# Spectral layer in three parts of 4, 2 and 2 channel blocks instead of two halves

## Chip, cores and metric

The kernel runs on one core of a Trainium2 chip. The metric is the device time of one execution in microseconds (us); the figure for a kernel is the median of its runs. Times inside an execution are counted from the start of the profiled span.

## What is computed

The input is an image of 48 x 48 tokens with 768 channels, in float32. Layer 0 is a transformer block (attention with relative positions, then an MLP). Layer 1, which the change touches, filters in the frequency domain, separately in 8 blocks of 96 channels. Cut to what matters:

```
xf = rfft2(x, axes=(1, 2), norm='ortho')          # 48 x 25 frequencies
xf = xf.reshape(B, H, Wh, 8, 96)
o1r = relu(mm(xr, w1[0]) - mm(xi, w1[1]) + b1[0])  # per block, 96 x 96
o1i = relu(mm(xi, w1[0]) + mm(xr, w1[1]) + b1[1])
o2r = softshrink(mm(o1r, w2[0]) - mm(o1i, w2[1]) + b2[0], 0.01)
o2i = softshrink(mm(o1i, w2[0]) + mm(o1r, w2[1]) + b2[1], 0.01)
y = irfft2((o2r + 1j * o2i).reshape(B, H, Wh, C), s=(H, W), norm='ortho')
return y + x
```

Blocks of channels do not mix, so the layer may be worked on in any groups of blocks. All frequencies of a block have to be there before its last transform along the rows.

## The kernel before

All Fourier transforms are matmuls with constant matrices. They run in four steps, with two trips through scratch memory in DRAM.

**Rows forward** (`rows_forward`, lines 1069 to 1087) runs at the end of each of the three passes `p` of the MLP. It multiplies the tokens in `x1` by `rows_dft` into PSUM (`zp`), copies them to an SBUF tile `zt` (eight buffers, 100 partitions x 384), and writes each `zt` to `z1[k]`, where `k` is the half of the channels. In the first two passes ScalarE makes the copies; in the last pass VectorE and ScalarE take turns (`balanced_copy`, lines 73 to 77). In the last pass the loads of the first two units (below) are issued between the writes of the two halves.

**Units** (`class Unit`, lines 1180 to 1279). The spectral part is cut into 14 units: two halves of 4 channel blocks, each with 7 groups of up to 4 column frequencies `k` (25 in all, so that the last unit of a half has only one). A unit passes through a load and four stages:

- `load`: `load_frequencies` (line 937) brings two `zi` tiles from `z1`, two frequencies each.
- `columns(i)`, frequency `i`: one matmul for each block into `fp`, and a copy to `xf` (VectorE for even `i`, ScalarE for odd).
- `first(i)`, block `i`: VectorE adds real and imaginary part (`both`), three 192-wide matmuls go into `lp` and `l1`, ScalarE copies `l1` (`p_both`), VectorE adds it (`pre`), ScalarE applies the relu (`o1`), and GpSimd writes a negated copy next to it.
- `second(i)`, frequency `i`: two matmuls for each block into `mp2`, VectorE adds the bias (`zz`) and clamps (`cl`), GpSimd subtracts `cl` from `zz`.
- `back(i)`, frequency `i`: one matmul into `yp`, as wide as the half (384), a copy to `y`; after each second frequency `y` is written to `z2`.

**Rows back** (`rows_back`, lines 1281 to 1297) is a generator for one half and one of six groups `g` of rows. Its first step loads `zo` (100 partitions, three buffers) from `z2`; each of the next three steps, called pieces here, makes two matmuls into `rps`, adds `x1` on VectorE into `yt` (four buffers), and writes `yt` to the output.

**Order.** The loop at line 1308 goes through rounds `r`, and in each round through steps `i` of 0 to 3. In a step stand `back` of unit `r-3`, `second` of `r-2`, `first` of `r-1` and `columns` of `r`, so four units are under way at once. From round 12 each step also advances the row generators of the first half: 20 of their 24 steps lie in the rounds, the other four behind the loop, and then come the six groups of the second half, one after the other. This order is binding for TensorE alone (`manual_schedule` at line 1306). The queues of the other engines, and that of SyncE, which issues all transfers of this part, are ordered by the framework; each runs its own queue in order. The framework also makes an instruction wait until a buffer it needs is free.

In the trace a float32 matmul has two records, so the 72 matmuls of the row step show as `x144`.

Of the kernel before, what the change touches and what calls it, by code (L numbers as in the profile page):

```python
# [9 lines left out]
F32 = mybir.dt.float32  # L10
# [3 lines left out]
ALU = mybir.AluOpType  # L14
# [4 lines left out]
P = 128  # L19
HW = 48  # L20
T = HW * HW
# [8 lines left out]
G = 384  # L30
NB = 8
BS = C // NB
CH = C // 2
KW = HW // 2 + 1
LAM = 0.01
LOW = -3.0e38
# [8 lines left out]
def block_then_afno(  # L45
# [25 lines left out]
    nc = tc.nc  # L71

    def balanced_copy(i, dst, src):
        if i % 2:
            nc.scalar.copy(dst, src)
        else:
            nc.vector.tensor_copy(dst, src)
# [14 lines left out]
    dram = ctx.enter_context(tc.tile_pool(name="scratch", bufs=1, space=DRAM))  # L92

    z1 = [dram.tile([HW * 2 * KW, CH], F32, name=f"z1_{k}") for k in range(2)]
    z2 = [dram.tile([HW * 2 * KW, CH], F32, name=f"z2_{k}") for k in range(2)]
    q_d = [dram.tile([P, T], F32, name=f"q_d{i}") for i in range(NC)]
    k_d = [dram.tile([P, T], F32, name=f"k_d{i}") for i in range(NC)]
    v_d = dram.tile([T, C], F32, name="v_d")
# [6 lines left out]
    x1 = main.rearrange("p (t c) -> p t c", t=NT)  # L105
# [83 lines left out]
    with ExitStack() as flag_scope:  # L189
# [11 lines left out]
        with ExitStack() as att:  # L201
# [336 lines left out]
            with tc.manual_schedule(engines={mybir.EngineType.PE, mybir.EngineType.SP}):  # L538
# [3 lines left out]
                psum = att.enter_context(tc.tile_pool(name="ps_att", bufs=1, space=PSUM))  # L542
# [76 lines left out]
                with tc.manual_schedule(engines={mybir.EngineType.Activation}):  # L619
                    for n, (pr, c, u) in enumerate(runs):  # L620
# [111 lines left out]
        with tc.If(safe < 1):  # L732
            with ExitStack() as att:
# [27 lines left out]
                for pr in range(NC):  # L761
                    w3 = []
                    for n, name in enumerate(("g_wq", "g_wk", "g_wv")):
                        w = w_pool.tile([P, NC, P], F32, name=name)
                        nc.sync.dma_start(
                            out=w,
# [167 lines left out]
    turn = ctx.enter_context(tc.tile_pool(name="turn", bufs=6))  # L934
    first_loads = []

    def load_frequencies(half, k0):

        rows = z1[half].rearrange("(r k) c -> r k c", k=KW)
        tiles = []  # L940
        for k in range(k0, min(k0 + 4, KW), 2):
            n = min(2, KW - k)
            zi = turn.tile([P, C], F32, name="zi", tag="turn")
            zi = zi[: 2 * HW].rearrange("p (k c) -> p k c", c=CH)
            nc.sync.dma_start(out=zi[:, :n], in_=rows[:, k : k + n, :])
            tiles.append(zi)
        return tiles

    with ExitStack() as mlp:
# [119 lines left out]
        def rows_forward(p):  # L1069

            for k in range(2):
                for g in (2 * p, 2 * p + 1):
                    for a, parts in enumerate(((0,), (1, 2), (3, 4), (5,))):
                        zp = psum.tile([2 * 2 * KW, CH], F32, name="zp", tag=f"o{a}")
                        for b in parts:
                            nc.tensor.matmul(  # L1076
                                zp, rows_dft[:, b, :], x1[:, 3 * g + b // 2, ts(k, CH)],
                                start=(b == parts[0]), stop=(b == parts[-1]),
                            )
                        zt = turn.tile([2 * 2 * KW, CH], F32, name="zt", bufs=8)  # L1080
                        if p < 2:
                            nc.scalar.copy(zt, zp)
                        else:
                            balanced_copy(a, zt, zp)
                        nc.sync.dma_start(out=z1[k][ts(4 * g + a, 4 * KW), :], in_=zt)
                if (p, k) == (2, 0):
                    first_loads.extend(load_frequencies(0, k0) for k0 in (0, 4))
# [39 lines left out]
    with ExitStack() as sp:  # L1127
# [44 lines left out]
        nc.vector.tensor_tensor(a1e, a1e, a1[:, 0], ALU.subtract)  # L1172

        z2_h = [z.rearrange("(r k) c -> r k c", k=KW) for z in z2]
        NBH = NB // 2

        def by_k(a):
            return a.rearrange("p (k h) -> p k h", h=HW)
# [1 line left out]
        class Unit:  # L1180
# [1 line left out]

            def __init__(self, half, k0):
                self.half, self.k0 = half, k0
                self.nk = min(4, KW - k0)
                self.n = self.nk * HW
                self.zz = []

            def load(self):
                self.zi = first_loads.pop(0) if first_loads else load_frequencies(self.half, self.k0)

            def columns(self, i):

                if i == 0:
                    self.xf = mid.tile([BS, NBH, 2, 4, HW], F32, name="xf")
                if i >= self.nk:
                    return
                fp = psum.tile([BS, NBH, 2, HW], F32, name="fp", tag="f")  # L1200
                for b in range(NBH):
                    nc.tensor.matmul(  # L1202
                        fp[:, b].rearrange("p t h -> p (t h)"), self.zi[i // 2][:, i % 2, ts(b, BS)], cols,
                        start=True, stop=True,
                    )
                balanced_copy(i, self.xf[:, :, :, i, :], fp)

            def first(self, i):

                if i == 0:  # L1210

                    self.o1 = mid.tile([BS, NBH, 4, 3, HW], F32, name="o1")
                b = NBH * self.half + i
                re, im = (
                    self.xf[:, i, t, : self.nk, :].rearrange("p k h -> p (k h)") for t in range(2)
                )
# [25 lines left out]
            def second(self, i):  # L1242

                if i >= self.nk:
                    return
                zz = mid.tile([2 * HW, NBH, BS], F32, name="zz", bufs=10)
                self.zz.append(zz)
                blocks_at = NBH * self.half
                mp = psum.tile([2 * HW, NBH, BS], F32, name="mp2", tag="m")
                for e in range(NBH):  # L1250
                    for t in range(2):
                        nc.tensor.matmul(  # L1252
                            mp[:, e], self.o1[:, e, i, 1 - t : 3 - t].rearrange("p t h -> p (t h)"),
                            a2[:, blocks_at + e, t], start=(t == 0), stop=(t == 1),
                        )
                nc.vector.tensor_tensor(zz, mp, d2[:, ds(blocks_at, NBH)], ALU.add)

                flat = zz.rearrange("p n o -> p (n o)")
                cl = mid.tile([2 * HW, CH], F32, name="cl", bufs=3)
                nc.vector.tensor_scalar(cl, flat, LAM, -LAM, ALU.min, ALU.max)  # L1260
                nc.gpsimd.tensor_tensor(flat, flat, cl, ALU.subtract)

            def back(self, i):

                if i >= self.nk:
                    return
                zz = self.zz[i]
                if i % 2 == 0:
                    self.y = mid.tile([2 * HW, 2, CH], F32, name="y", bufs=3)
                yp = psum.tile([2 * HW, CH], F32, name="yp", tag="y", bufs=1)  # L1270
                nc.tensor.matmul(  # L1271
                    yp, icols, zz.rearrange("p n o -> p (n o)"), start=True, stop=True
                )
                balanced_copy(i, self.y[:, i % 2, :], yp)
                if i % 2 or i == self.nk - 1:
                    n = i % 2 + 1
                    nc.sync.dma_start(
                        out=z2_h[self.half][:, ds(self.k0 + i + 1 - n, n), :], in_=self.y[:, :n]
                    )

        def rows_back(half, g):

            zo = zin.tile([4 * KW, 4, CH], F32, name="zo", bufs=3)
            nc.sync.dma_start(
                out=zo, in_=z2[half][ts(g, 16 * KW), :].rearrange("(a p) c -> p a c", a=4)
            )
            yield
            for i in range(3):
                yt = mid.tile([P, CH], F32, name="yt", bufs=4)
                rp = psum.tile([P, CH], F32, name="rps", tag="f")  # L1290
                for e in range(2):
                    nc.tensor.matmul(  # L1292
                        rp, irows[:, 2 * i + e, :], zo[:, i + e, :], start=(e == 0), stop=(e == 1)
                    )
                nc.vector.tensor_tensor(yt, rp, x1[:, 3 * g + i, ts(half, CH)], ALU.add)
                nc.sync.dma_start(out=out[ts(3 * g + i, P), ts(half, CH)], in_=yt)
                yield

        units = [Unit(half, k0) for half in range(2) for k0 in range(0, KW, 4)]
        ends = [[rows_back(half, g) for g in range(T // G)] for half in range(2)]  # L1300

        def pieces(gens):
            for gen in gens:
                yield from gen

        with tc.manual_schedule(engines={mybir.EngineType.PE}):
            first_half = pieces(ends[0])
            for r in range(len(units) + 3):
                if r < len(units):
                    units[r].load()  # L1310
                for i in range(4):
                    for stage, lag in (("back", 3), ("second", 2), ("first", 1), ("columns", 0)):
                        if 0 <= r - lag < len(units):
                            getattr(units[r - lag], stage)(i)
                    if r > len(units) // 2 + 4:
                        next(first_half, None)
            for _ in first_half:
                pass
            for _ in pieces(ends[1]):
                pass  # L1320


def _constants():
# [125 lines left out]
```

## Time and profile before

| | |
|---|---|
| runs, us | 2924.24, 2926.68, 2931.56; median 2926.68 |
| profiled execution, us | 2924.9 (its span 2922.9) |
| granted clock of TensorE | 0.998 |
| last rows-forward stage | 2656 to 2672 us of the span |
| rounds | 2672 to 2881 us |
| first matmul of the last `back` | 2880.50 us |
| only row steps left | 2881 to 2920 us |
| row matmuls (`rps`) | 144 records, 50.3 us busy |
| `zo` loads | 12 of 600 KB |
| `z1` to `zi` loads | 24 of 288 KB, 2 of 144 KB |
| `z2` writes | 24 of 288 KB, 2 of 144 KB |
| output writes | 36 of 192 KB |

The page lists the busy time of each engine: PE is TensorE's matmuls, PEld its weight loads (which overlap), DVE is VectorE, ACT ScalarE, POOL GpSimd, SP SyncE. A view of stages gives the busy time of each engine between two points in time, then the granted clock, the mean busy share of the 16 DMA engines, and what they moved. The chain of waits is followed back from the last instruction: at each step to what released it. In a list of instructions the bracket says how long the engine had been idle and what it waited for last.

### The profile page before, as it was taken

The numbers are of one execution on the slowest core, as the hardware profiler recorded it, in microseconds if no ns is written. First come the engines' busy times: TensorE is split into PE (matmuls) and PEld (weight loads), VectorE is DVE, ScalarE is ACT, GpSimd is POOL, SyncE is SP. The second block draws the span as 40 slices with busy tenths as digits, with TensorE's granted clock in tenths as the row PEclk, the third lists the DMA queues.
The fourth block names the chain that finished last, engine by engine and source line by source line (L and its number), as shares of the span: only waits on it lengthen the run. The fifth ranks groups of instructions, "written<-read, shape, count | busy, mean of one in ns | idle before, by whom it ended". The sixth has DMA issues, their size and how long they took to land. (4 is left out here: it accounts for less than half of the span.)

```text
span 2922.9 us, 40961 instructions
## 1 busy us (share of the span) xinstructions
PE 2864.6 (98%) x15659; PEld 1724.2 (59%) x15659; DVE 1791.0 (61%) x2606; ACT 936.3 (32%) x1514; POOL 609.8 (21%) x564
## 2 busy tenths in 40 slices
PE   7999999999999999999999999999999999999998
PEld 4555665555555555555555555555555555556885
DVE  5243237777777777777733666674666566665564
ACT  1011126656666565665500211122011211102331
POOL 2302110000000000000043322343332323222441
PEclk9999999999999999999999999999999999999999
DMA  3423276173462716435252111212121212113235
GB/s 127 148 88 118 92 162 123 30 135 64 82 128 41 144 34 101 109 59 87 56 177 76 43 56 53 65 64 65 57 65 54 77 54 65 54 57 99 79 93 179
DMA packets 202818, 253.03 MB, mean 87 GB/s; under 512 B 21618, under 2 KB 180978, under 8 KB 201078
## 3 DMA queue, kind: packets, MB, share of 16 engines
q1 hardware_dynamic: 202614, 250.32, 33.5%
q8 instruction: 126, 2.06, 0.3%
q14 instruction: 78, 0.64, 0.1%
HBM read 136.40 MB, written 50.14 MB: 64 GB/s over the span
## 5 line engine op out<-in xcount | busy, mean ns | idle before, releaser
L635 DVE TENSOR_TENSOR acc<-acc,main 128x768 f32<-128x768 f32 x576 | 551.9, 958 | 206.4 <-ACT main L569 149.9
L569 ACT ACTIVATE main<-sp 128x768 f32<-128x768 f32 x648 | 520.8, 812 | 138.9 <-PE sp L565 132.2
L565 PE MATMUL sp<-terms,select 64*128 64x384 f32 x1296 | 413.3, 630 | 0.0
L1051 DVE TENSOR_TENSOR main<-o,main 128x384 f32<-128x384 f32 x540 | 299.4, 557 | 40.3 <-PE o L1049 2.1
L989 PE MATMUL h<-shared,w 128*128 128x384 f32 x864 | 296.7, 486 | 0.8 <-issue 0.8
L559 PE MATMUL sp<-shared 64*128 64x384 f32 x1296 | 268.0, 490 | 2.5 <-DVE o L457 2.2
L559 PE MATMUL sp<-qT,kT 64*128 64x384 f32 x1296 | 266.7, 487 | 0.2
L612 POOL TENSOR_TENSOR inverse<-inverse,rden 128x384 f32<-128x384 f32 x36 | 46.3, 1287 | 1010.7 <-DVE rden L609 918.1
L446 PE MATMUL m<-main 128*128 128x384 f32 x756 | 247.0, 488 | 6.4 <-DVE rstd L121 3.0
L989 PEld LDWEIGHTS h<-shared,w 128*128 128x128 f32 x864 | 164.4, 190 | 116.1 <-issue 2.3
L989 PE MATMUL h<-shared,w1s 128*128 128x384 f32 x648 | 226.6, 486 | 0.0
L582 PE MATMUL op<-main,shared 128*64 128x384 f32 x1296 | 221.2, 488 | 0.0
L582 PE MATMUL op<-main,v 128*64 128x384 f32 x1296 | 219.9, 488 | 0.0
L995 ACT ACTIVATE hT<-c,vec 128x384 f32<-128x384 f32 x108 | 66.4, 615 | 466.2 <-DVE c L1001 466.1
L446 PEld LDWEIGHTS m<-main 128*128 128x128 f32 x756 | 142.6, 190 | 108.3 <-issue 8.7
L1001 DVE TENSOR_TENSOR c<-h,u 128x384 f32<-128x384 f32 x108 | 60.2, 557 | 212.3 <-PE h L989 212.3
L1049 PE MATMUL o<-w,hT 128*128 128x384 f32 x432 | 175.0, 487 | 3.0 <-DVE mv L118 2.0
L1049 PE MATMUL o<-w2s,hs 128*128 128x384 f32 x432 | 174.8, 487 | 3.1 <-DVE hs L155 3.1
L565 PEld LDWEIGHTS sp<-terms,select 64*128 64x128 f32 x1296 | 125.8, 187 | 83.9 <-issue 0.5
L989 PEld LDWEIGHTS h<-shared,w1s 128*128 128x128 f32 x648 | 123.1, 190 | 85.9
L154 POOL TENSOR_TENSOR w1s<-w 128x384 f32<-128x384 f32 x36 | 36.4, 1010 | 610.9 <-PE o L1049 289.4
L559 PEld LDWEIGHTS sp<-shared 64*128 64x128 f32 x1296 | 117.9, 187 | 61.3 <-issue 23.1
(158 smaller groups left out, 3896.8 us busy)
## 6 DMA issues: line engine op xcount, KB each, us to landing
w<-in_mlp_w_dram SPq DMA_DIRECT2D x72, 768.0 KB
terms<-col_parts SPq DMA_DIRECT2D x432, 72.0 KB
terms<-row_hi SPq DMA_DIRECT2D x216, 72.0 KB
terms<-row_lo SPq DMA_DIRECT2D x216, 72.0 KB
main<-in_qkv_w_dram SPq DMA_DIRECT2D x36, 384.0 KB
z<-zt SPq DMA_DIRECT2D x48, 150.0 KB
zo<-z SPq DMA_DIRECT2D x12, 600.0 KB
x<-in_x_dram SPq DMA_DIRECT2D x18, 384.0 KB
```

Of the source, the lines that this page charges most:

```text
L446: nc.tensor.matmul(bank, a[:, c, :], b[:, c, :], start=(first and c == 0), stop=(c == 2), skip_group_check=not first,)
L559: nc.tensor.matmul(sp[:, j, :G], kT[at, ts(kt, P)], qT[at, ts(c, G)], start=True, stop=False,)
L565: nc.tensor.matmul(sp[:, j, :G], select[at, a % 2], ready[pr, c][at, a // 2, b], start=False, stop=True,)
L569: nc.scalar.activation(p, sp[:, :, :G], AF.Exp, scale=HD**-0.5)
L582: nc.tensor.matmul(op[ts(j, 64)], v[:, kt0 + i, ts(j, 64)], ps[i][:, j, :], start=(kt0 + i == 0), stop=(kt0 + i == NT - 1),)
L612: nc.gpsimd.tensor_tensor(inverse, inverse, rden, ALU.add)
L635: nc.vector.tensor_tensor(acc, made[0] if kt == 1 else acc, p, ALU.add)
L989: nc.tensor.matmul(bank[i], a[:, c, :], b[:, c, :], start=(start and c == 0), stop=(c == 2), skip_group_check=not start,)
L995: nc.scalar.activation(h[:, i, ts(k, G)], src, AF.Gelu, bias=col(V_B1 + 2 * n + i))
L1001: nc.vector.tensor_tensor(t, src, other, ALU.add)
L1049: nc.tensor.matmul(bank[k], a, b, start=start, stop=True, skip_group_check=not start)
L1051: nc.vector.tensor_tensor(dst, bank[k], dst, ALU.add)
```

## The change

The two halves become three parts: blocks 0 to 3, 4 and 5, 6 and 7. There are now 21 units, seven for each part, and each stage works on the blocks of its part only (`self.nb`); for a part of two blocks `first` does nothing at i = 2 and 3. `z2` is laid out in three tensors of 384, 192 and 192 columns. `z1` stays as it is, and the smaller parts read half of its rows' width. Tiles in SBUF and PSUM keep their full size, and the smaller parts use a slice.

The row steps of a part are now one generator, `in_turn`: its first step loads the first two groups, and behind the three pieces of a group it issues the load of the group two ahead. Part 0's generator begins at step 3 of round 10 and makes its 18 pieces in steps 0 to 2 of rounds 11 to 16; part 1's begins at step 3 of round 18 and goes on from round 19. The loop ends with round 23, so that 15 of part 1's 18 pieces lie in the rounds; its other three and all of part 2's follow behind.

In `rows_forward` the four `zt` of a group become slices of one tile with two buffers in all; the space and the four writes stay as they were.

```diff
+PARTS = (0, 4), (4, 2), (6, 2)
...
-    z2 = [dram.tile([HW * 2 * KW, CH], F32, name=f"z2_{k}") for k in range(2)]
+    z2 = [
+        dram.tile([HW * 2 * KW, n * BS], F32, name=f"z2_{k}")
+        for k, (_, n) in enumerate(PARTS)
+    ]
...
-    def load_frequencies(half, k0):
+    def load_frequencies(part, k0):
...
-        rows = z1[half].rearrange("(r k) c -> r k c", k=KW)
+        block, n = PARTS[part]
+        k, c = divmod(block * BS, CH)
+        rows = z1[k].rearrange("(r k) c -> r k c", k=KW)
...
-            zi = zi[: 2 * HW].rearrange("p (k c) -> p k c", c=CH)
-            nc.sync.dma_start(out=zi[:, :n], in_=rows[:, k : k + n, :])
+            zi = zi[: 2 * HW, : 2 * n * BS].rearrange("p (k c) -> p k c", k=2)
+            nc.sync.dma_start(out=zi[:, :nk], in_=rows[:, k : k + nk, ds(c, n * BS)])
...
+                    zt4 = turn.tile([P, 4, CH], F32, name="zt", bufs=2)
...
-                        zt = turn.tile([2 * 2 * KW, CH], F32, name="zt", bufs=8)
+                        zt = zt4[: 2 * 2 * KW, a]
...
-                for b in range(NBH):
+                for b in range(self.nb):
...
-                balanced_copy(i, self.xf[:, :, :, i, :], fp)
+                balanced_copy(i, self.xf[:, : self.nb, :, i, :], fp[:, : self.nb])
...
+                if i >= self.nb:
+                    return
+                b = self.block + i
...
-        def rows_back(half, g):
+        def rows_back(part, g):
...
-            zo = zin.tile([4 * KW, 4, CH], F32, name="zo", bufs=3)
+            block, n = PARTS[part]
+            zo = zin.tile([4 * KW, 4, CH], F32, name="zo", bufs=3)[:, :, : n * BS]
...
-        def pieces(gens):
-            for gen in gens:
-                yield from gen
+        def in_turn(part):
+
+            gens = [rows_back(part, g) for g in range(T // G)]
+            for gen in gens[:2]:
+                next(gen)
+            yield
+            for g, gen in enumerate(gens):
+                for _ in range(3):
+                    next(gen)
+                    yield
+                for later in gens[g + 2 : g + 3]:
+                    next(later)
+
+        units = [Unit(part, k0) for part in range(len(PARTS)) for k0 in range(0, KW, 4)]
+        ends = [in_turn(part) for part in range(len(PARTS))]
+        per = len(units) // len(PARTS)
...
-                    if r > len(units) // 2 + 4:
-                        next(first_half, None)
-            for _ in first_half:
-                pass
-            for _ in pieces(ends[1]):
-                pass
+
+                    for part in range(len(PARTS) - 1):
+                        begin = per * (part + 1) + 3 + part
+                        if (r, i) == (begin, 3) or (begin < r <= begin + 6 and i < 3):
+                            next(ends[part])
+            for part in ends:
+                for _ in part:
+                    pass
```

More of the change, by code (lines that the diff above doesn't have):

```diff
@@ L935, in block_then_afno @@
     first_loads = []
-    def load_frequencies(half, k0):
-        rows = z1[half].rearrange("(r k) c -> r k c", k=KW)
+    def load_frequencies(part, k0):
+        block, n = PARTS[part]
+        k, c = divmod(block * BS, CH)
+        rows = z1[k].rearrange("(r k) c -> r k c", k=KW)
         tiles = []
         for k in range(k0, min(k0 + 4, KW), 2):
-            n = min(2, KW - k)
+            nk = min(2, KW - k)
             zi = turn.tile([P, C], F32, name="zi", tag="turn")
-            zi = zi[: 2 * HW].rearrange("p (k c) -> p k c", c=CH)
-            nc.sync.dma_start(out=zi[:, :n], in_=rows[:, k : k + n, :])
+            zi = zi[: 2 * HW, : 2 * n * BS].rearrange("p (k c) -> p k c", k=2)
+            nc.sync.dma_start(out=zi[:, :nk], in_=rows[:, k : k + nk, ds(c, n * BS)])
             tiles.append(zi)
@@ L1174, in block_then_afno @@
         z2_h = [z.rearrange("(r k) c -> r k c", k=KW) for z in z2]
-        NBH = NB // 2
+        NBH = PARTS[0][1]
         def by_k(a):
@@ L1180, in block_then_afno, with __init__ @@
         class Unit:
-            def __init__(self, half, k0):
-                self.half, self.k0 = half, k0
+            def __init__(self, part, k0):
+                self.part, self.k0 = part, k0
+                self.block, self.nb = PARTS[part]
                 self.nk = min(4, KW - k0)
@@ L1191, in load @@
             def load(self):
-                self.zi = first_loads.pop(0) if first_loads else load_frequencies(self.half, self.k0)
+                self.zi = first_loads.pop(0) if first_loads else load_frequencies(self.part, self.k0)
             def columns(self, i):
@@ L1212, in first @@
                     self.o1 = mid.tile([BS, NBH, 4, 3, HW], F32, name="o1")
-                b = NBH * self.half + i
+                if i >= self.nb:
+                    return
+                b = self.block + i
                 re, im = (
@@ L1245, in second @@
                     return
-                zz = mid.tile([2 * HW, NBH, BS], F32, name="zz", bufs=10)
+                zz = mid.tile([2 * HW, NBH, BS], F32, name="zz", bufs=10)[:, : self.nb]
                 self.zz.append(zz)
-                blocks_at = NBH * self.half
-                mp = psum.tile([2 * HW, NBH, BS], F32, name="mp2", tag="m")
-                for e in range(NBH):
+                mp = psum.tile([2 * HW, NBH, BS], F32, name="mp2", tag="m")[:, : self.nb]
+                for e in range(self.nb):
                     for t in range(2):
@@ L1253, in second @@
                             mp[:, e], self.o1[:, e, i, 1 - t : 3 - t].rearrange("p t h -> p (t h)"),
-                            a2[:, blocks_at + e, t], start=(t == 0), stop=(t == 1),
+                            a2[:, self.block + e, t], start=(t == 0), stop=(t == 1),
                         )
-                nc.vector.tensor_tensor(zz, mp, d2[:, ds(blocks_at, NBH)], ALU.add)
+                nc.vector.tensor_tensor(zz, mp, d2[:, ds(self.block, self.nb)], ALU.add)
                 flat = zz.rearrange("p n o -> p (n o)")
-                cl = mid.tile([2 * HW, CH], F32, name="cl", bufs=3)
+                cl = mid.tile([2 * HW, CH], F32, name="cl", bufs=3)[:, : self.nb * BS]
                 nc.vector.tensor_scalar(cl, flat, LAM, -LAM, ALU.min, ALU.max)
@@ L1269, in back @@
                     self.y = mid.tile([2 * HW, 2, CH], F32, name="y", bufs=3)
+                    self.y = self.y[:, :, : self.nb * BS]
                 yp = psum.tile([2 * HW, CH], F32, name="yp", tag="y", bufs=1)
+                yp = yp[:, : self.nb * BS]
                 nc.tensor.matmul(
@@ L1277, in back @@
                     nc.sync.dma_start(
-                        out=z2_h[self.half][:, ds(self.k0 + i + 1 - n, n), :], in_=self.y[:, :n]
+                        out=z2_h[self.part][:, ds(self.k0 + i + 1 - n, n), :], in_=self.y[:, :n]
                     )
-        def rows_back(half, g):
-            zo = zin.tile([4 * KW, 4, CH], F32, name="zo", bufs=3)
+        def rows_back(part, g):
+            block, n = PARTS[part]
+            zo = zin.tile([4 * KW, 4, CH], F32, name="zo", bufs=3)[:, :, : n * BS]
             nc.sync.dma_start(
-                out=zo, in_=z2[half][ts(g, 16 * KW), :].rearrange("(a p) c -> p a c", a=4)
+                out=zo, in_=z2[part][ts(g, 16 * KW), :].rearrange("(a p) c -> p a c", a=4)
             )
@@ L1288, in rows_back @@
             for i in range(3):
-                yt = mid.tile([P, CH], F32, name="yt", bufs=4)
-                rp = psum.tile([P, CH], F32, name="rps", tag="f")
+                yt = mid.tile([P, CH], F32, name="yt", bufs=4)[:, : n * BS]
+                rp = psum.tile([P, CH], F32, name="rps", tag="f")[:, : n * BS]
                 for e in range(2):
@@ L1294, in rows_back @@
                     )
-                nc.vector.tensor_tensor(yt, rp, x1[:, 3 * g + i, ts(half, CH)], ALU.add)
-                nc.sync.dma_start(out=out[ts(3 * g + i, P), ts(half, CH)], in_=yt)
+                at = ds(block * BS, n * BS)
+                nc.vector.tensor_tensor(yt, rp, x1[:, 3 * g + i, at], ALU.add)
+                nc.sync.dma_start(out=out[ts(3 * g + i, P), at], in_=yt)
                 yield
-        units = [Unit(half, k0) for half in range(2) for k0 in range(0, KW, 4)]
-        ends = [[rows_back(half, g) for g in range(T // G)] for half in range(2)]
-        def pieces(gens):
-            for gen in gens:
-                yield from gen
+        def in_turn(part):
[12 more added lines that the diff above has]
+        per = len(units) // len(PARTS)
         with tc.manual_schedule(engines={mybir.EngineType.PE}):
-            first_half = pieces(ends[0])
             for r in range(len(units) + 3):
```

## The prediction

> **What bounds the kernel now.** I read the page first, then busy time by stage over the last 270 us, then the chain of waits there, then the order of instructions in the last 50 us, with SyncE's queue and the DMA packets.
>
> ```profile
> PE 2864.6 (98%) x15659; PEld 1724.2 (59%) x15659; DVE 1791.0 (61%) x2606; ACT 936.3 (32%) x1514; POOL 609.8 (21%) x564
> ```
>
> TensorE is busy almost throughout, so only its gaps can be won. The change touches the time after 2656 us. By stage (PE, PEld, DVE, ACT, POOL busy, clock, DMA share, GB/s):
>
> ```profile
> 2695.00:2742.00 47.00, 45.80 (x397) 41.33 (x396) 28.28 (x62) 18.26 (x50) 21.73 (x25) 1.00 0.25 73
> 2827.00:2861.00 34.00, 34.00 (x252) 28.07 (x250) 19.64 (x44) 11.17 (x30) 13.51 (x16) 1.00 0.29 87
> 2890.00:2923.00 33.00, 24.65 (x72) 13.16 (x72) 10.60 (x19) 0.00 (x0) 0.00 (x0) 0.99 0.66 215
> ```
>
> The rounds are TensorE's with small holes; the last 33 us are not: TensorE idles, and DMA moves 215 GB/s. The chain of waits in a round, then at the end:
>
> ```profile
> 2707.62 0.65 PE yp L1271 x2
> 2708.27 1.36 PE mp L1252 x16
> 2710.60 0.69 PE fp L1202 x8
> 2711.79 0.71 ACT o L1234 x2
> 2712.58 0.89 POOL o L1238
> 2714.90 0.68 PE fp L1202 x8
> ...
> 2881.31 6.17 PE rps L1292 x20
> 2887.49 6.80 DMA zo<-z
> 2894.42 3.87 PE rps L1292 x12
> 2898.29 7.30 DMA zo<-z
> 2905.73 3.87 PE rps L1292 x12
> 2909.60 5.73 DMA zo<-z
> ```
>
> In a round the chain leaves TensorE once, for ScalarE and GpSimd finishing the last block's `o1`. At the end it alternates between 3.87 us of matmuls and a load of `zo`. The order of instructions adds a second wait there: VectorE for an output transfer to free one of four `yt`.
>
> ```profile
> 2890.02 4.11 PE L1292 MATMUL rps<-zo,shared 100*128 100x384 f32 x12 [0.96 <-DMA zo<-z]
> 2890.38 0.56 DVE L1295 TENSOR_TENSOR yt<-rps,main 128x384 f32<-128x384 f32 x1 [2.02 <-DMA out_dram<-yt]
> 2894.92 0.56 DVE L1295 TENSOR_TENSOR yt<-rps,main 128x384 f32<-128x384 f32 x1 [1.49 <-DMA out_dram<-yt]
> ```
>
> **Landmarks before.** The last `back` starts its matmul at 2880.50. Then: `z2` write issued 2881.93, first `zo` load of the second half issued 2883.88, its first row matmul 2890.02 (9.52 us in all, of which first-half row pieces cover 8.4). Six groups follow; starts from 2890.02 to 2915.47 give 5.09 us a group, where matmuls need 12 x 0.3225 = 3.87. The last `yt` ends 2920.17 (30.15 after 2890.02), and the span ends 2.73 later. Sum 9.52 + 30.15 + 2.73 = 42.4.
>
> **TensorE's own work.** Every matmul keeps its columns. A 384-wide matmul takes two records of 0.3225; two 192-wide records take 0.3255 (`lp`). So `yp` (25 more matmuls) and `rps` (36 more) add 25 x 0.0065 + 36 x 0.006 = about 0.3 us. What moves: before, 84 row records follow the last `back`, 27.1 us. After, part 0 (18 pieces of 1.29) and 12 pieces of part 1 (0.65) lie inside the rounds, 3 + 3 pieces of part 1 and 18 of part 2 behind the last `back`: 24 x 0.651 = 15.6. The last `back` starts 27.1 - 15.6 + 0.3 = 11.8 us later by this.
>
> **Waits in the rounds.** From the end of `first(3)` on TensorE (2710.44) to the start of the last `mp` pair (2713.51) the `o1` chain takes 3.07 us; fp 0.68, yp 0.65 and fourteen mp records 1.19 cover 2.52, and a step that is 3.66 elsewhere takes 4.30: 0.64 lost. In a two-block round `first` has only i = 0, 1; after it come fp 0.34, two steps of 0.325 + 0.68 + 0.34 = 1.35, yp 0.325 and mp 0.34: 3.7 against 3.07, no wait. Part 0 keeps its six; the second half's four (at 2781.65, 2794.99, 2810.27 whole, 2825.35 about 0.44) go: 3 x 0.64 + 0.44 = 2.4 us won. So the last `back` comes 9.4 later.
>
> **What hides the added small work.** Added: 25 more each of `xf` copies, `zz`, `cl`, `y` and GpSimd's subtraction, 18 more `yt`. A two-block round takes TensorE 4 x 1.35 + 2 x 0.98 = 7.3 us. VectorE, with 0.355 for 192 columns from PSUM (between 0.254 for 96 and 0.554 for 384) and 0.27 for `cl` (between 0.18 and 0.355): 4 x 0.355 + 4 x 0.27 + 4 x 0.355 + 2 x (0.373 + 0.554) = 5.8. ScalarE 3.7; GpSimd, 0.6 per subtraction (0.51 to 1.0) and 0.71 per negation, 3.8. All below 7.3: cost nothing, unless VectorE's order delays the hand-over between rounds (rival D). There cover shrinks most: yp and mp before `first(0)` fall from 2.0 to 1.0 us.
>
> **SyncE.** Issues grow by 13 `zi`, 13 `z2`, 6 `zo`, 18 `out`, 50 of about 0.32 us: 16 us over 240, eight per round at most, 2.6 of 9.3 us. Before, loads of `zi` were issued up to three units ahead (the last at 2800.74, used at 2845.16); three two-block units are still 22 us. In the tail four issues, 1.3 us, lie beside 1.95 of matmuls. Cost nothing.
>
> **The `zt` tile.** A copy may now wait for transfers five copies back instead of eight. In the last rows stage four copies take 3.87 us; the fourth `z1` write of k = 0's second group must have landed before the thirteenth copy at 2668.37. SyncE issues the `zi` loads, which need just these writes, at 2666.83, so it had: 1.5 us spare. In the two earlier stages sixteen writes go out in 15.1 and 16.0 us, in step with the copies. Zero; if the spare were gone, each later group would wait some 1 us, bound +2.
>
> **The tail.** From the last `back`: issue of the `z2` write after 1.43 - 0.32 (half the matmul) - 0.2 (half the copy) = 0.9. The 144 KB write took 1.95; I keep it, though 72 KB now move. The first `zo` load (600 KB, now 300) took 6.14: between 3.07 if bytes decide and 6.14 if none of it does; I take 4.0, since other transfers before it halve as well. Row matmuls start at 6.9; row pieces cover 4.2, so TensorE waits 2.7 (before 1.1). Then the period of a group. Lower bound: matmuls, 6 x 0.3255 = 1.95. Upper: 5.09, if nothing scales. Transfers in 2890 to 2920: 69.3% of 16 engines over 30 us by 4404 packets above 512 B, 75.5 ns per 1536 B; a 3072 B packet took 162 ns (2695 to 2742: 24.9%, 1152 packets), so time goes with bytes and half-size packets about halve it: 2.55 by 5.09/2. The wait for `yt` has a part that does not halve: an output came back after 5.9 and 6.56 us, a lone write after 1.95. (6.2 - 1.95)/2 + 1.95 + 0.36 for VectorE, over four buffers, is 1.11 per piece, 3.3 a group. Between 2.55 and 3.3, nearer bytes, because loads now go out two and three groups ahead: 2.8. Five periods and 2.4 for the last group: 16.4. End of span 2.5 after (2.73 less a quarter of a microsecond for half the bytes). Sum 6.9 + 16.4 + 2.5 = 25.8.
>
> [...]
>
> **Sum.** 9.4 + 25.8 - 42.4 = -7.2 us. The profiled execution took 2924.9 (span 2922.9), so 2917.7; the median before is 1.8 above it, so I forecast 2919.5. With periods of 2.2 to 3.3 and a microsecond of scatter: 2915.5 to 2923.
>
> **Rivals.**
> A, the forecast.
> B, the tail becomes TensorE's: 1.95 a group and the first load in 3.1: -7.2 - 4.25 - 0.9 = -12.3, 2914.4. For it: loads issued ahead. Against: 588 KB in 1.95 us is 301 GB/s, and the tail moves 215 to 227.
> C, the end is hidden no better: a period of 4.0, the first load in 6.1, queued behind the outputs of part 1 on SyncE (their last VectorE addition is 1.9 us later than the `z2` landing): -7.2 + 6.0 + 2.1 + 1.9 = +2.8, 2929.5. For it: before, loads stood behind outputs (issued 2893.88 behind four).
> D, slower: at each hand-over VectorE runs `zz` and `cl` before the next `both`. With cover of 1.0 and VectorE 79% full that costs 0.5 us a round, up to a whole step's VectorE work, 1.45. Over 14 units: 7 to 20; at the upper end -7.2 + 20 = +12.8, 2939.5. It decides from 7.2/14 = 0.51 a round, and shows as slower from 1.14. Against: at 2711.82 VectorE ran `both` as soon as `xf` was there.
>
> **Chances.** A 0.46 (0.12 of it below 2917.9), B 0.26, C 0.12, D 0.16 (0.04 of it within the bound). What this kernel's measurement can tell from no change is about 0.3%, 8.8 us: 2917.9 to 2935.5. Faster 0.12 + 0.26 = 0.38; same 0.34 + 0.12 + 0.04 = 0.50; slower 0.12. The range 2913 to 2930 takes in A, B and C; outside it lie D and some hundredths of B.
>
> **What would show it.** Right: 192-wide row groups 2.2 to 3.3 us apart, first `zo` load within 4.5 us, no POOL wait of `mp` in two-block rounds, 25 to 27 us from the last `yp` to the end. Wrong: TensorE waiting for `xf` or `both` in each two-block round, groups 4 us apart, or ScalarE waiting for `zt` transfers.

## The result and the profile after

| | before | after |
|---|---|---|
| median of 20 runs each, us | 2928.77 | 2933.57 |
| ratio, 95% interval | | 1.0019 (1.0013 to 1.0025) |
| profiled execution (its span), us | 2924.9 (2922.9) | 2934.77 (2932.9) |
| last `zp` record to last `back` (its second `yp` record), us | 209.7 | 227.6 |
| from there to the last VectorE row addition, us | 38.8 | 29.1 |
| that addition to the end, us | 3.3 | 3.2 |

The kernel became about 5 us slower: less than the 8.8 us that I had called measurable, but the interval lies clear of 1. The span of the profiled execution grew by 10.0 us, of which 1.9 lie before the last `zp` record, up to which nothing of the change but the `zt` tile is at work (that record stands at 2671.1 and at 2673.0 us). From that record on it is +8.1: the last `back` comes 17.9 us later, and only 9.8 come back behind it. Single executions scatter by several microseconds (2929.91 to 2938.30 over the twenty after), so the table says where time lies, and the ratios how much it is.

The first view of the page after, busy time by engine:

```profile
PE 2872.9 (98%) x15781; PEld 1747.7 (60%) x15781; DVE 1802.1 (61%) x2700; ACT 940.7 (32%) x1538; POOL 617.5 (21%) x589
```

TensorE has 122 more records, as counted (50 of `yp`, 72 of `rps`), but is busy for 8.3 us more, where narrower matmuls should cost 0.3. The order of TensorE's instructions shows where: two places in the rounds, then the end (start, duration, the instruction, and in the bracket the idle time with what ended it).

```profile
2775.87 0.50 PE L1210 MATMUL fp<-shared,zi 96*96 96x96 f32 x4
2776.68 0.89 PE L1282 MATMUL yp<-zz,shared 96*96 96x384 f32 x2 [0.31 <-DVE y L78]
2777.40 0.50 PE L1210 MATMUL fp<-shared,zi 96*96 96x96 f32 x4
2778.22 0.86 PE L1282 MATMUL yp<-zz,shared 96*96 96x384 f32 x2 [0.32 <-ACT y L76]
...
2900.43 0.54 PE L1282 MATMUL yp<-zz,shared 96*96 96x192 f32 x2 [0.54 <-ACT y L76]
2900.80 4.20 PE L1304 MATMUL rps<-zo,shared 100*128 100x192 f32 x24
2908.71 9.29 PE L1304 MATMUL rps<-zo,shared 100*128 100x192 f32 x36 [3.70 <-DMA zo<-z]
2918.49 2.29 PE L1304 MATMUL rps<-zo,shared 100*128 100x192 f32 x12 [0.50 <-DVE yt L1308]
2921.22 2.31 PE L1304 MATMUL rps<-zo,shared 100*128 100x192 f32 x12 [0.44 <-DMA zo<-z]
2925.45 4.18 PE L1304 MATMUL rps<-zo,shared 100*128 100x192 f32 x12 [1.93 <-DMA zo<-z]
```

Twelve row records take 2.29 us at 2918 and 4.18 at 2925; the 36 at 2908 take 9.29, though the 24 at 2900 took 4.20. The view by stage says why (busy us of PE, PEld, DVE, ACT and POOL, then the granted clock, DMA share, GB/s):

```profile
2901.00:2905.00 4.00, 4.00 (x24) 3.46 (x22) 1.79 (x5) 0.00 (x0) 0.00 (x0) 1.00 0.39 113
2905.00:2909.00 4.00, 0.30 (x2) 0.32 (x2) 0.62 (x2) 0.00 (x0) 0.00 (x0) 0.89 0.60 181
2909.00:2912.00 3.00, 3.00 (x10) 3.00 (x10) 0.72 (x2) 0.00 (x0) 0.00 (x0) 0.50 0.70 224
2912.00:2915.00 3.00, 3.00 (x11) 3.00 (x11) 0.71 (x2) 0.00 (x0) 0.00 (x0) 0.51 0.26 80
2915.00:2918.00 3.00, 3.00 (x18) 2.48 (x16) 1.07 (x3) 0.00 (x0) 0.00 (x0) 1.00 0.66 199
2925.00:2930.00 5.00, 4.18 (x12) 3.70 (x12) 1.05 (x3) 0.00 (x0) 0.00 (x0) 0.52 0.16 52
```

After TensorE had stood idle for 3.70 us its clock was half for about six microseconds: 10 or 11 records in 3 us where 18 fit at 1.00. At 2925 it was half again. TensorE looks fully busy in these rows; the clock column must be read before the busy one.

Why it stood idle: SyncE's queue after the last `back` (issues and the time they took).

```profile
2900.34 1.39 SPq L1288 DMA_DIRECT2D z<-y  x2
2902.04 2.85 SPq L1309 DMA_DIRECT2D out_dram<-yt  x3
2905.06 0.31 SPq L1296 DMA_DIRECT2D zo<-z  x1
2905.46 1.56 SPq L1309 DMA_DIRECT2D out_dram<-yt  x3
2907.08 0.96 SPq L1296 DMA_DIRECT2D zo<-z  x2
```

The last `z2` write was issued at 2901.4, and by the semaphore records of the trace it had landed at 2903.0. But the first load of part 2 went out only at 2905.06, 2.1 us later, behind three outputs, each of which waits for VectorE. The row matmuls began 3.65 us after that.

### The profile page after: what moved, and what is told of

Read it like the earlier page. It is cut to its first block, busy times and chain, and to the rows that moved or that the text cites. A ratio compares the mean times of both kernels' runs of the same rounds, so it can differ in the third digit from the quotient of the medians.

```text
span 2932.9 us, 41567 instructions
## 1 busy us (share of the span) xinstructions
PE 2872.9 (98%) x15781; PEld 1747.7 (60%) x15781; DVE 1802.1 (61%) x2700; ACT 940.7 (32%) x1538; POOL 617.5 (21%) x589
```

## The experiments

My first theory after the result: the cover in front of the last part got too small, TensorE idles, and its clock drops. Rivals: small transfers make the tail slow; waits in the rounds cost the time; the `zt` tile does. All ratios are to the kernel before on the same chip.

**Fill the idle stretch.** Six extra matmuls, whose result nobody reads, stand in front of part 2's rows:

```diff
             for part in ends:
+                if part is ends[-1]:
+                    for _ in range(6):
+                        idle = psum.tile([2 * HW, CH], F32, name="idle", tag="l1", bufs=1)
+                        nc.tensor.matmul(
+                            idle, icols, d2[:, 0:4].rearrange("p n o -> p (n o)"),
+                            start=True, stop=True,
+                        )
```

> The changed kernel with six extra matmuls (icols times a slice of d2, 0.65 us each, result unused) between the last row piece of part 1 and the first of part 2, in the stretch in which TensorE sat idle for 3.7 us before 2908.71. Theory G: the idle stretch is what halves TensorE's granted clock (0.89, 0.50, 0.51 from 2905 to 2915), and the slow matmuls delay the loads behind them. Then the clock stays at 1.00 over the first three groups of part 2, nine pieces take about 6 instead of 9.3 us, and the time falls by 3 us: about 2.5 us above the kernel before (ratio 1.001) instead of 5.5 (1.0019). Rival D (the transfers of zo and yt set the pace of the tail whatever the clock): the clock stays up, but the pieces wait for transfers instead and the ratio stays at 1.0019; if the fillers run into the arrival of zo, 1.002.

Measured: 1.0008 (1.0000 to 1.0017), against 1.0019 for the change alone; last `back` to last addition 25.5 instead of 29.1 us. TensorE's order:

```profile
2905.42 5.53 PE L1346 MATMUL idle<-shared 96*96 96x384 f32 x12
2910.78 2.18 PE L1304 MATMUL rps<-zo,shared 100*128 100x192 f32 x12
2913.25 3.62 PE L1304 MATMUL rps<-zo,shared 100*128 100x192 f32 x20 [0.28 <-DMA zo<-z]
```

The fillers run past the time at which the load is there, so the first row matmul comes later than without them (9.8 us behind the last `back`, before 8.3). Yet twelve records take 2.2 us again, and the clock stays at 1.00 to the last matmul. So in this stretch it was the idle time that halved the clock (0.50 and 0.51 from 2909 to 2915 with it), and with the clock up the tail is shorter although the fillers do nothing: the halved clock is a cause of lost time, not a mark of the wait. How much it is worth is known roughly, about 3 us, since the intervals of the two ratios still touch.

**Part 2's loads on ScalarE's queue**, which has nothing else to do by then:

```diff
-            nc.sync.dma_start(
+            queue = nc.scalar if part == len(PARTS) - 1 else nc.sync
+            queue.dma_start(
```

> The changed kernel with the six zo loads of part 2 issued from ScalarE's queue (idle there) instead of SyncE's, where the first stood behind three output writes. Theory Q (queue position): the first load is issued when the last z2 write has landed, 1.7 us earlier, the first row matmul of part 2 follows 1.7 us earlier, TensorE idles 2.0 instead of 3.7 us, and by theory G the clock may then stay at 1.00: 1.7 us less without and up to 5 us less with that, ratio 1.0013 down to 1.0002. Rival D (transfers set the pace): the loads start earlier but share the same DMA engines with the outputs, the end does not move, ratio 1.0019.

Measured: 1.0008 (0.9999 to 1.0017); the second stretch falls to 23.7 us. TensorE's order, then ScalarE's queue:

```profile
2903.12 4.52 PE L1305 MATMUL rps<-zo,shared 100*128 100x192 f32 x16 [2.17 <-DMA zo<-z]
2907.85 2.94 PE L1305 MATMUL rps<-zo,shared 100*128 100x192 f32 x16 [0.22 <-DVE yt L1309]
...
2898.98 13.77 ACTq L1297 DMA_DIRECT2D zo<-z  x6
```

The idle time falls from 3.70 to 2.17 us; the clock still dips (0.85 and 0.81 in the two 5 us after 2900). The queue order is thus worth 1.5 us of the stall. What stops TensorE next is VectorE, waiting for output buffers.

**Two parts again**, with the other edits of the change kept:

```diff
-PARTS = (0, 4), (4, 2), (6, 2)
+PARTS = (0, 4), (4, 4)
```

> The changed kernel with PARTS = (0, 4), (4, 4): two halves again, but with the new order of row steps, loads two groups ahead, and the zt tile of four. Theory H (what stands behind the last back matters): only 3 pieces of 1.29 us and the last back's 0.65 cover the 9.5 us until the first zo has landed, so TensorE idles about 5 us (1.1 before) and its clock halves there; part of this comes back as the groups follow each other 4.8 instead of 5.09 us apart; the waits of yp for y are gone: 4 to 7 us above the kernel before, ratio 1.0014 to 1.0024. Rival S (the split in small parts is what costs, by its short rounds): ratio 1.000 or below, since loads go out earlier.

Measured: 1.0026 (1.0016 to 1.0036). TensorE's order:

```profile
2888.02 4.04 PE L1304 MATMUL rps<-zo,shared 100*128 100x384 f32 x12
2897.28 14.29 PE L1304 MATMUL rps<-zo,shared 100*128 100x384 f32 x36 [5.22 <-DMA zo<-z]
```

Only three pieces (4.04 us) of part 0 are left as cover, since the new schedule finishes a part's rows earlier; the wait is 5.22 us, and 36 records that take 11.6 at full clock (36 x 0.3225) take 14.29. The parts' widths are as before and the transfers large, and it is still no faster than the change itself (the intervals overlap). So small transfers are not needed to make the tail slow; too little work behind the last `back` is enough.

**Single `zt` buffers again**, eight of them:

```diff
-                    zt4 = turn.tile([P, 4, CH], F32, name="zt", bufs=2)
-                        zt = zt4[: 2 * 2 * KW, a]
+                        zt = turn.tile([2 * 2 * KW, CH], F32, name="zt", bufs=8)
```

> The changed kernel with zt as before (eight single buffers instead of two of four). All theories but one: no difference from the changed kernel, ratio 1.0019, zp to fp gap 0.74 us in both. Rival Z (the coarser buffer costs in the three rows stages): some 2 us less, ratio 1.0012.

Measured: 1.0017 (1.0008 to 1.0025), that is the change's own ratio within its interval. The tile costs nothing that these runs can tell.

**Two PSUM banks for `yp`**, taken from `lp`:

```diff
-                lp = psum.tile([BS, 2, 4 * HW], F32, name="lp", tag="l")
+                lp = psum.tile([BS, 2, 4 * HW], F32, name="lp", tag="l", bufs=1)
-                yp = psum.tile([2 * HW, CH], F32, name="yp", tag="y", bufs=1)
+                yp = psum.tile([2 * HW, CH], F32, name="yp", tag="y", bufs=2)
```

> The changed kernel with two PSUM banks for yp instead of one, and one for lp instead of two. Theory Y: in the changed kernel yp waits for the copy to y because back follows back with too little between (0.17, 0.47, 0.48 us in round 9, 0.15 and 0.36 in round 16, 0.18 and 0.54 in rounds 22 and 23); with a second bank these 2.3 us go, nothing waits for lp: ratio 1.0011. Rival: the waits move to another place, since ScalarE's copies come late in its queue (1.2 us after the matmul in the trace): ratio 1.0019.

Measured: 1.0011 (1.0002 to 1.0020); the last `back` comes 0.8 us earlier (226.8). The waits of `yp` are gone, but `lp` now waits three times, 1.0 us in all by the brackets, for VectorE. The interval overlaps that of the change: no more than some tenths of a microsecond to 2 us lie here.

**Part 1's rows begin two rounds later**, so that more of them stand behind the last `back`:

```diff
-                        begin = per * (part + 1) + 3 + part
+                        begin = per * (part + 1) + 3 + 3 * part
```

> The changed kernel with part 1's row pieces begun two rounds later (begin of part 1 at round 20 instead of 18): nine pieces stay behind the loop instead of three. They are the same pieces, only moved past the last back, so they cover 0.33 + 12 x 0.65 = 8.1 us of the 8.3 from the last back's matmul to the first row matmul of part 2. Theory G: TensorE's idle stretch shrinks from 3.7 us to under 1, the clock stays at 1.00; 3 us of waiting and 3 of slow matmuls go: ratio 0.9998 (0.9990 to 1.0007). Rival D (transfers set the pace of the tail): the outputs of the moved pieces lie in the same DMA queues as the loads, the tail is longer by what the loop is shorter, ratio 1.0015 to 1.002.

Measured: 1.0012 (1.0003 to 1.0022), a miss: at most part of the gain forecast came, and the interval overlaps that of the change. The last `back` comes 3.4 us earlier (224.2), but the second stretch grows to 30.6: part 1's last loads now also stand behind outputs on SyncE, and TensorE waits for `zo` five times (0.99, 1.24, 0.99, 1.30, 2.21 us). Here more cover, without a queue of its own for the loads, mostly moved the waits.

**Loads on ScalarE's queue and seven output buffers** (`yt` from 4 to 7, `zz` from 10 to 7 to make room):

```diff
-                zz = mid.tile([2 * HW, NBH, BS], F32, name="zz", bufs=10)[:, : self.nb]
+                zz = mid.tile([2 * HW, NBH, BS], F32, name="zz", bufs=7)[:, : self.nb]
-            nc.sync.dma_start(
+            queue = nc.scalar if part == len(PARTS) - 1 else nc.sync
+            queue.dma_start(
-                yt = mid.tile([P, CH], F32, name="yt", bufs=4)[:, : n * BS]
+                yt = mid.tile([P, CH], F32, name="yt", bufs=7)[:, : n * BS]
```

> The changed kernel with part 2's zo loads on ScalarE's queue and seven yt instead of four (zz has seven instead of ten, so that it fits). Beside e2_loads_act, whose groups followed each other about 2.9 us apart and whose VectorE waited 0.2 to 2 us for an output to free a yt. Theory B (buffers): with seven the groups come 2.0 to 2.4 us apart, 2 to 3 us less, ratio 1.0000. Rival D (DMA engines): the period stays, ratio 1.0008.

Measured: 1.0003 (0.9993 to 1.0013). With both, the three parts draw level with the two halves, no more. TensorE's order:

```profile
2909.63 13.71 PE L1305 MATMUL rps<-zo,shared 100*128 100x192 f32 x60 [2.30 <-DMA zo<-z]
```

Five groups run without a gap, but the mean clock from 2903.0 to the end was 0.87, and the 60 records took 13.71 us where the last kernel below has 36 in 6.53 at 1.00; so part of what the buffers give does not show. The ratio alone does not decide against rival D of this run, whose 1.0008 lies in the interval.

**The same edits on the kernel before**, its two halves kept:

```diff
-                zz = mid.tile([2 * HW, NBH, BS], F32, name="zz", bufs=10)
+                zz = mid.tile([2 * HW, NBH, BS], F32, name="zz", bufs=7)
-            nc.sync.dma_start(
+            queue = nc.scalar if half else nc.sync
+            queue.dma_start(
-                yt = mid.tile([P, CH], F32, name="yt", bufs=4)
+                yt = mid.tile([P, CH], F32, name="yt", bufs=7)
```

> The kernel before with the second half's zo loads on ScalarE's queue and seven yt (zz seven). Rival D (DMA engines set the 5.09 us of a 384-wide group): the period falls to 4.8 at most, ratio 0.9993 to 1. Theory B (buffers and queue order): it falls towards the 3.87 us of the matmuls, 5 us less, ratio 0.998.

Measured: 0.9973 (0.9962 to 0.9983), median 2921.63 us: faster than both kernels. TensorE's order at the end:

```profile
2883.38 7.90 PE L1293 MATMUL rps<-zo,shared 100*128 100x384 f32 x24
2892.50 4.11 PE L1293 MATMUL rps<-zo,shared 100*128 100x384 f32 x12 [1.22 <-DMA zo<-z]
2897.09 4.11 PE L1293 MATMUL rps<-zo,shared 100*128 100x384 f32 x12 [0.48 <-DMA zo<-z]
2901.47 15.72 PE L1293 MATMUL rps<-zo,shared 100*128 100x384 f32 x48 [0.27 <-DMA zo<-z]
```

The last four groups run with no gap in 15.72 us, 3.87 a group, where before they came 5.09 apart. The transfers in this kernel from 2892 to 2912:

```profile
DMA packets 4025, 5.79 MB, mean 290 GB/s; under 512 B 274, under 2 KB 4022, under 8 KB 4022
```

and in the kernel before, from 2890 to 2915:

```profile
DMA packets 4187, 6.02 MB, mean 241 GB/s; under 512 B 285, under 2 KB 4184, under 8 KB 4184
```

The packets are alike, 20% more bytes pass per microsecond: the DMA engines were not what bounded the tail of before.

**Each of the two alone on the kernel before.** The buffers:

```diff
-                zz = mid.tile([2 * HW, NBH, BS], F32, name="zz", bufs=10)
+                zz = mid.tile([2 * HW, NBH, BS], F32, name="zz", bufs=7)
-                yt = mid.tile([P, CH], F32, name="yt", bufs=4)
+                yt = mid.tile([P, CH], F32, name="yt", bufs=7)
```

> The kernel before with seven yt (zz seven), loads left on SyncE. It parts e9_before_act_yt7's gain (0.9973). If free yt were what the groups waited for: all of it, 0.9975. If it was the place of the loads in SyncE's queue, behind outputs: no gain, 1.000.

The queue:

```diff
-            nc.sync.dma_start(
+            queue = nc.scalar if half else nc.sync
+            queue.dma_start(
```

> The kernel before with the second half's zo loads on ScalarE's queue, four yt. If the place in SyncE's queue was what the groups waited for: 0.9975. If it was yt: 1.000 to 0.9995, since the loads come earlier but VectorE still waits for outputs. If both are needed, half of e9_before_act_yt7's gain here and little in e10_before_yt7.

Measured: buffers alone 1.0001 (0.9992 to 1.0010), queue alone 0.9986 (0.9974 to 0.9998), both 0.9973 (0.9962 to 0.9983). The queue alone gains; the buffers alone do not. That the buffers add to the queue is likely but not settled by the ratios, whose intervals overlap. The traces speak for it: behind the last `back` VectorE waited for an output to free a `yt` twice (3.5 us in all) in the kernel before, ten times (12.8 us) with the queue alone, and once (0.7 us) with both. The buffers' profile also shows the clock: after a wait of 3.52 us it was 0.57 between 2920 and 2925.

**Everything on the three parts**: part 1 begins later, two `yp` banks, seven `yt`, and the loads of the last groups of part 1 and all of part 2 on ScalarE's queue:

```diff
+            queue = nc.scalar if 6 * part + g > 9 else nc.sync
-                        begin = per * (part + 1) + 3 + part
+                        begin = per * (part + 1) + 3 + 3 * part
...
```

> The three parts with the remedies together: part 1's row pieces begun at round 20, the last two zo loads of part 1 and all of part 2 on ScalarE's queue, seven yt (zz seven), two PSUM banks for yp and one for lp. Theory G with B: no idle stretch over 2 us behind the last back, clock 1.00 there, groups of part 2 2.0 to 2.4 us apart. Worked out from the traces: last back at 224.2 - 0.8 after the last rows-forward matmul (as in e6_later less the gain of e5_y2), 8.1 to the first row matmul of part 2, 12 to 14 for its groups, 3.3: 247 to 249, against 251.8 for the kernel before and 247.4 for e9_before_act_yt7. Ratio 0.9985 to 0.9975. Rival S (the split costs of itself, whatever stands behind the last back): above 1.000.

Measured: 0.9998 (0.9990 to 1.0007), a miss: I had expected 0.9985 to 0.9975. TensorE's order, and the transfers of its tail (2900 to 2917):

```profile
2900.94 6.53 PE L1305 MATMUL rps<-zo,shared 100*128 100x192 f32 x36 [0.70 <-DMA zo<-z]
2908.62 6.65 PE L1305 MATMUL rps<-zo,shared 100*128 100x192 f32 x36 [1.16 <-DMA zo<-z]
2916.67 2.26 PE L1305 MATMUL rps<-zo,shared 100*128 100x192 f32 x12 [1.40 <-DMA zo<-z]
```

```profile
DMA packets 5758, 4.12 MB, mean 242 GB/s; under 512 B 431, under 2 KB 5756, under 8 KB 5756
```

The clock stays at 1.00 here and the queue is free, but each third group waits for its load: groups come 2.6 us apart where matmuls need 1.95. With 768 B packets the DMA engines, busy for 76% of the time, move 242 GB/s; the two halves with queue and buffers moved 290 with 1536 B packets at 79%. So of two kernels with these two cures the one with large transfers ends 2.5 per thousand lower (0.9998 against 0.9973, each against the kernel before on its own chip). Why is not shown. The kernel before, with 1536 B packets, also moved only 241 GB/s at 75%, so a low rate does not by itself show that packets are too small; and a wait at each third group also fits the three `zo` buffers, which now hold half as much. Neither was tried by itself.

## Why the prediction was wrong

I forecast -7.2 us from the last rows-forward stage on; the profile shows +8.1. Of the 15.3 between them 8.6 lie before the last `back` and 6.7 behind it (counted, as in the forecast, from its first record; the table above counts from the second).

**"What moves" was miscounted: 3.9 us.** I put 84 row records behind the last `back` before the change. They are 24 + 6 x 12 = 96, 31.0 us. The order of before has 24 and then six groups; the 48 others lie in the rounds:

```profile
2880.50 0.81 PE L1271 MATMUL yp<-zz,shared 96*96 96x384 f32 x2
2881.15 7.90 PE L1292 MATMUL rps<-zo,shared 100*128 100x384 f32 x24
```

The last `back` thus moves by 31.0 - 15.6 + 0.3 = 15.7 us, not 11.8.

**The waits in the rounds: 4.7 us.** I took off 2.4 for the wait of `mp` on GpSimd. That wait did shrink. The waits of before, then of after (total us, times, longest):

```profile
PE mp L1252 <- POOL o L1238: 3.7, 10, 0.4
```

```profile
PE mp L1261 <- POOL o L1248: 2.5, 7, 0.4
PE yp L1282 <- ACT y L76: 1.2, 4, 0.5
```

It went from ten times to seven, one more than the six I had reckoned with; the seventh, at 2771.46, is in the round in which the first two-block unit follows the four-block ones. But a wait that I had put at nothing came: `yp` has one PSUM bank, and where the new parts meet the old one (2776 and 2778 above) or run out (2898, 2900), too little stands between two `back` to cover the copy to `y`. Starting points show that the two at 2776 and 2778 cost 0.16 us more than their brackets: an `fp` group is 0.50 long, but where nothing waits the next matmul starts 0.34 after it, and a bracket counts only from its end. Counted this way, against the usual spacing of each kind of matmul, the delays of `mp` fell by 2.0 us (6.9 to 4.9), those of `yp` rose by 3.1 from almost nothing, those of the row matmuls by 0.7, and the matmuls' own spacing makes 16.0 us instead of 15.7. All told the last `back` came 18.0 us later instead of 15.7: +2.3 where I had -2.4. The run with two banks shows that the single bank causes the `yp` delays: there none is left, though `lp`, down to one bank, takes back 2.3 of the 3.1 us.

**The tail, 25.8 forecast, 32.5 measured.** The first row matmul came 8.3 us after the last `back` (forecast 6.9). From the issue of the load to the matmul it took 3.65 (forecast 4.0), but the load was issued 2.1 us after the write it needs had landed; that is close to the 1.9 of rival C, to which I gave 0.12. In the forecast SyncE "cost nothing" because I priced the time of its issues and not their order. The five periods took 16.7 (forecast 14.0), and from the last group to the end 7.5 (forecast 4.9). Of these last 5.3 us the halved clock is the greater part: its records took 3.1 and 1.9 us longer, and keeping the clock up gained 3.2 us by the ratio. The second of the two belongs to this execution: in the profiles with single `zt` and with two `yp` banks, which have the same row steps, the last twelve records took 2.26 and 2.25 us. No step of mine had a clock in it, though the working itself said TensorE would wait 2.7 us there.

**"Time goes with bytes" was wrong as a bound.** I took 5.09 us a group as what transfers allow, and halved it. The same transfers run at 3.87. The 5.09 were a loop through SyncE's queue:

```profile
2888.39 5.40 SPq L1296 DMA_DIRECT2D out_dram<-yt  x4
2893.88 0.32 SPq L1284 DMA_DIRECT2D zo<-z  x1
```

A load stands behind outputs, an output waits for VectorE, VectorE for matmuls (and twice for a free `yt`), and the matmuls for an earlier load. 75.5 ns a packet had waiting in it: by the same reckoning it is 68 ns in the two halves with queue and buffers (79.2% of 16 engines over 20 us, 3748 packets above 512 B). The semaphore records of before show one landing at 2884.35 and ten from 2889.3 to 2889.9 for the load issued at 2883.88 (100 partitions), and sixteen for an output (128); what that means for the time of a transfer is not shown.

Whether halved transfers move their bytes at a lower rate is not settled: with queue and buffers they did (242 against 290 GB/s), but the whole ones of before reached only 241. The last `z2` write, 72 KB, landed 1.6 us after its issue, where I had kept the 1.95 of 144 KB. The period of a group was 3.3 us (forecast 2.8), and 2.6 in the last kernel. (Rival B's 301 GB/s is 309, since the profile's KB has 1024 bytes; this moves nothing.)

**What held.** A steady two-block round took 7.33 us (2855.71 to 2863.04), forecast 7.3. The small work added on VectorE, ScalarE and GpSimd, and SyncE's 50 issues, cost nothing visible in them; rival D did not appear. VectorE took 0.35 for 192 columns and 0.26 for `cl`, GpSimd 0.61. The `zt` tile cost nothing that could be told.

## What to carry to other kernels

Before you halve the transfers of a tail, ask whether the DMA engines or the order of one issuing queue set its pace: put the loads on a queue that waits for nothing, give the outputs more buffers, and see whether the gaps close (here 5.09 us a group became 3.87). When work is moved from behind the last dependent step into the busy part, count exactly what is left behind it as cover, since an idle stretch on TensorE costs its own length and can be followed by a slower clock, as the 3.70 us here were by 0.50. A single PSUM bank that was covered by a wide neighbour needs a second look when that neighbour becomes half as wide (here 3.1 us of delays of `yp`).

## What was not expected of the hardware

The granted clock fell to half after an idle stretch of 3.70 us in the change (0.50 from 2909 to 2912), and 36 narrow records then took 9.29 us, where the last kernel has 36 in 6.53 at 1.00. After 5.22 us (two parts) the clock was 0.54 from 2895 to 2900 and 0.78 from 2900 to 2905; after 3.52 us (buffers alone) it was 0.75 from 2915 to 2920 and 0.57 from 2920 to 2925. Shorter stretches went both ways. With one of 2.30 us (loads on ScalarE's queue, seven `yt`) the mean from 2903.0 to the end was 0.87; one of 2.17 us was followed by 0.85 and 0.81 over five microseconds each, and one of 1.93 us in the tail of the change by 0.52. But with two `yp` banks, behind 1.99 us, twelve records took 2.25 us, no more than the 2.29 of twelve at 1.00 (2918 to 2921 in the change):

```profile
2926.55 2.25 PE L1304 MATMUL rps<-zo,shared 100*128 100x192 f32 x12 [1.99 <-DMA zo<-z]
```

Stretches of 0.3 to 1.6 us in the kernel before left the clock at 1.00 (2890 to 2920). So near 2 us the length of the last stretch does not decide; what does is not shown here.

Moving loads to another issuing engine gained 4.4 us (2925.54 against 2929.90). Together with more buffers it raised the tail's rate from 241 to 290 GB/s, since a load no longer queued behind stores that waited for another engine.
